# Recommendation scoring on one core: target rows fetched one by one from SyncE instead of by 128 indirect gathers on GpSimd

## Chip, cores and metric

The kernel runs on one core of a Trainium2 chip. The metric is the device time of one execution in microseconds (us). The median of 3 runs of the kernel before is 36,285.59 us (36,284.45 to 36,299.23).

## The reference

All arithmetic is in float32. There are 50,001 items, 16,384 users, and 100 history items for each user.

```python
def _neighbor_attn(E, near_full):                 # E: 50001 x 32
    V = E[near_full]                              # 32 neighbours of each item
    scores = jnp.einsum('nd,nkd->nk', E, V) / jnp.sqrt(jnp.float32(GEO_HALF))
    w = jax.nn.softmax(scores, axis=-1)
    return jnp.einsum('nk,nkd->nd', w, V)
...
a_sus = _neighbor_attn(E_in, near_full)
a_inf = _neighbor_attn(E_out, near_full)
hist_bi = jnp.concatenate([a_sus[history], a_inf[history]], axis=-1)
tgt_bi = jnp.concatenate([a_inf[target], a_sus[target]], axis=-1)
h = jnp.concatenate([E_hist[history], hist_bi], axis=-1)    # 16384 x 100 x 128
t = jnp.concatenate([E_tgt[target], tgt_bi], axis=-1)       # 16384 x 128
x = h * t[:, None, :]
z = jax.nn.relu(jnp.einsum('bld,hd->blh', x, W1) + b1)
scores = jnp.einsum('blh,h->bl', z, W2[0])
exp_A = jnp.exp(scores)
mask = (history != target[:, None]) & (history != 0)
exp_A = exp_A * mask
denom = jnp.sum(exp_A, axis=-1) ** BETA
attn = exp_A / denom[:, None]
result = h * attn[..., None]
s = jnp.sum(result)
...                                               # cosine of the vector (s, ..., s) and t
return jax.nn.sigmoid(pred)
```

## The kernel before

There are two stages, one behind the other, and both are paced by indirect gathers that GpSimd (POOL) issues. An indirect gather takes a column of 128 item numbers from SBUF and fetches one row of a DRAM table into each of the 128 partitions.

The first stage works out the neighbour attention of all items, 128 items at a time, with 32 gathers for each (L136), and writes two tables to DRAM: `table`, a row for an item as history (its sum and 128 values), and `ttab`, a row for an item as target (128 float32 values, 512 bytes; the first half is copied from the input at the very start, L104 and L105, and the second half is written by ScalarE's queue at the end of each block, L230).

The second stage scores the users. User number p x 128 + c lies in partition p of column c, so that the targets, loaded once as `tidx`, are a tile of 128 x 128 with the users' columns side by side, and `tidf` is the same in float32. There are 128 columns of 128 users. A column has 25 groups of four history positions. The order of the work is written out by hand (`tc.manual_schedule`) for all five engines, and each engine goes through its own work in that order:

- `history_of(i)` loads the histories of four columns from SyncE (SP), L292. There are 4 buffers.
- `target_rows(c)` fetches the target rows t of a column, L296. It is called for the first column ahead of the loop, and for each next column at group 5 of the one before. There are 3 buffers of t.
- `gather(s)` issues the four gathers of group s into one of HBUF = 20 buffers of `h`, L332.
- `turn(s)` transposes the four on PE, L346, and `times_target(s)` multiplies with the transposed target rows on DVE, L351, and sets the rows' sums aside, L354. When both have read a buffer of h, it is free for the gathers of group s + 20.
- `hidden` and `scored` are the two matrix products (L363, L372), three and six groups later, with the ReLU on ScalarE between them (L365).
- `target_work(c + 1)` transposes the next column's t on PE (L308), copies it (L310), sums it (L312) and its squares (L314), and makes the mask; it stands behind group 15 of column c. On PE, all groups that follow stand behind the transpose of t.
- `kept`, `turned_back`, `weights` and `ended` close a column.

SP's part of the second stage is the history loads alone: two ahead of the loop, and one at each fourth column.

Of the kernel before, what the change touches and what calls it, by code (L numbers as in the profile page):

```python
# [10 lines left out]
F32 = mybir.dt.float32  # L11
I32 = mybir.dt.int32
U8 = mybir.dt.uint8
E = mybir.EngineType
AF = mybir.ActivationFunctionType
ALU = mybir.AluOpType
AX = mybir.AxisListType

P = 128
ITEMS = 50001  # L20
# [3 lines left out]
D = 128  # L24
# [17 lines left out]
UC = B // P  # L42
# [3 lines left out]
W = 1 + D  # L46
LAG = 3
HBUF = 20

@with_exitstack
def kernel(
# [13 lines left out]
    nc = tc.nc  # L67
# [4 lines left out]
    const = ctx.enter_context(tc.tile_pool(name="const", bufs=1))  # L72
# [5 lines left out]
    ttab = dram.tile([ROWS, D], F32, name="ttab")  # L78

    ident = const.tile([P, P], F32, name="ident")  # L80
# [25 lines left out]
    with (  # L106
# [7 lines left out]
        its = {}  # L114
# [151 lines left out]
    tidx = const.tile([P, UC], I32, name="tidx")  # L266
    nc.scalar.dma_start(tidx, target.rearrange("(p c) -> p c", p=P))
    tidf = const.tile([P, UC], F32, name="tidf")
    nc.vector.tensor_copy(tidf, tidx)
    with (  # L270
        tc.manual_schedule(engines={E.PE, E.Activation, E.DVE, E.SP, E.Pool}),
        tc.tile_pool(name="u_1", bufs=1) as u_1,
        tc.tile_pool(name="u_in", bufs=4) as u_in,
        tc.tile_pool(name="u_t", bufs=3) as u_t,
        tc.tile_pool(name="u_h", bufs=HBUF) as u_h,
        tc.tile_pool(name="u_x", bufs=6) as u_x,
# [16 lines left out]

        def target_rows(c):
            t = u_t.tile([P, D], F32, name="t")
            nc.gpsimd.indirect_dma_start(  # L296
                out=t,
                out_offset=None,
                in_=ttab[0:ITEMS, :],
                in_offset=bass.IndirectOffsetOnAxis(ap=tidx[:, c : c + 1], axis=0),  # L300
            )
            users[c] = {"t": t, "hidx": hists[c // BSUB][:, c % BSUB, :]}

        def target_work(c):
# [103 lines left out]
        history_of(0)  # L408
        history_of(1)
        target_rows(0)  # L410
        target_work(0)
        for s in range(last + 2 * LAG + 8):
            c, g = divmod(s, NG)
            if s < last:
                if g == 0 and c % BSUB == 2 and 0 < c // BSUB and c // BSUB + 1 < UC // BSUB:
                    history_of(c // BSUB + 1)
                if g == 5 and c + 1 < UC:
                    target_rows(c + 1)
                gather(s)
                turn(s)  # L420
                times_target(s)
            if 0 <= s - LAG < last:
                hidden(s - LAG)
            if 0 <= s - 2 * LAG < last:
                scored(s - 2 * LAG)
            if s < last and g == 15 and c + 1 < UC:
                target_work(c + 1)
            done, left = divmod(s - 2 * LAG - NG, NG)
            if 0 <= done < UC and left == 0:
                kept(done)  # L430
            if 0 <= done < UC and left == 2:
                turned_back(done)
            if 0 <= done < UC and left == 4:
                weights(done)
            if 0 <= done < UC and left == 6:
                ended(done)

    with (
# [12 lines left out]
        s = f_s.tile([P, 1], F32, name="s")  # L451
# [72 lines left out]
```

## Time and profile before

| | |
|---|---|
| median of 3 runs | 36,285.59 us |
| span of the profiled execution, first to last instruction | 31,861.9 us |
| first stage, to the change at about | 15,690 us |
| POOL busy | 24,005.6 us, 75% of the span |
| PE busy | 11,868.8 us, 37% of the span, all but 0.5 us of it in the second stage |
| gathers on POOL | 12,512 (L136), 12,800 (L332), 128 (L296) |
| TensorE clock granted, mean | 0.905 |

The page gives the span of the profiled execution and no time of that execution beyond it; the runs' times are those of other executions, without the profiler. Lines are those of the kernel before. A group of instructions is given as: line, engine, operation, output and inputs, count; then busy time in us and the mean of one in ns; then the idle time of that engine just before these instructions, and what ended it. Instructions that issue transfers, load registers or branch are not counted as busy; SP and the queues of the other engines (SPq, ACTq) appear in the timeline and among the waits only.

### The profile page before, as it was taken

Reading aid. Unit: us, or ns where it says so; the run is one execution under the profiler, and the core shown is the slowest. Engines: PE = TensorE matmul, PEld = TensorE weight load, DVE = VectorE, ACT = ScalarE, POOL = GpSimd, SP = SyncE. Lnnn points to the kernel's source line nnn. Section 1 sums busy time; section 2 is a strip of 40 time slices with the busy share of each in tenths; the row PEclk is TensorE's granted clock in tenths of the full one; section 3 lists DMA queues with packets and bytes.
Section 4 is the critical chain, followed back from the end, with each engine's and each line's share of the span. In section 5 each row is a group of like instructions: output and inputs, shape, how many; then the busy total and the mean of one; then the engine's idle time right before and its main releaser. Section 6 shows DMA issues by size and latency. Waiting matters only on the chain.

```text
span 31861.9 us, 106268 instructions
## 1 busy us (share of the span) xinstructions
PE 11868.8 (37%) x26243; PEld 3178.4 (10%) x26243; DVE 6716.4 (21%) x11111; ACT 2745.2 (9%) x6067; POOL 24005.6 (75%) x25446
## 2 busy tenths in 40 slices
PE   0000000000000000000277777777777777777777
PEld 0000000000000000000011111111111111111111
DVE  2222222222222222222211111111111111111111
ACT  0000000000000000000011111111111111111111
POOL 7777777777777777777777777777777777777777
PEclk9999999999999999999988888888888888888888
DMA  2111111111111111111122222222222222222222
GB/s 50 30 30 30 30 31 33 30 30 30 30 31 33 30 30 30 30 31 31 37 54 54 54 54 54 54 54 54 54 54 54 54 54 54 54 54 54 54 53 52
DMA packets 1027971, 1362.44 MB, mean 43 GB/s; under 512 B 559904, under 2 KB 614432, under 8 KB 1027360
## 3 DMA queue, kind: packets, MB, share of 16 engines
q0 software_dynamic: 814080, 1265.42, 19.7%
q10 hardware_dynamic: 151056, 51.51, 1.0%
q1 hardware_dynamic: 62224, 38.72, 0.5%
q8 instruction: 217, 3.56, 0.0%
q14 instruction: 394, 3.23, 0.0%
HBM read 1315.31 MB, written 51.50 MB: 43 GB/s over the span
## 4 chain that ended last, share of the span: by engine, by line
POOL 56%; issue 27%; DMA 9%; PE 7%; DVE 1%; POOLq 0%; ACT 0%; ACTq 0%; SPq 0%; DVEq 0%
POOL v L136 35%; POOL h L332 21%; DMA h<-table,hidx 6%; PE turned L372 3%; DMA v<-in_egeo_dram,nidx 3%; PE z_ps L363 3%; PE hT_ps L346 1%; POOL t L296 0%; DVE xT L351 0%; DVE ea L404 0%; DVE den L403 0%; DVE num L405 0%; DVE ea L402 0%; DVE hsum L354 0%; DMA table<-row 0%
## 5 line engine op out<-in xcount | busy, mean ns | idle before, releaser
L332 POOL DMA_INDIRECT h<-table,hidx x12800 | 12080.4, 944 | 3901.8 <-issue 3587.3
L136 POOL DMA_INDIRECT v<-in_egeo_dram,nidx x12512 | 11803.8, 943 | 3860.2 <-issue 3723.3
L308 PE MATMUL hT_ps<-ident,t 128*128 128x128 f32 x128 | 46.7, 365 | 15689.8 <-DMA hidx<-in_history_dram 15689.8
L346 PE MATMUL hT_ps<-ident,h 128*128 128x128 f32 x12800 | 3926.4, 350 | 4284.2 <-DMA h<-table,hidx 4186.4
L351 DVE TENSOR_TENSOR xT<-hT_ps,tT 128x512 f32<-128x512 f32 x3200 | 2213.9, 692 | 13113.0 <-PE hT_ps L346 13109.7
L372 PE MATMUL turned<-z,w_row 128*25 128x512 f32 x6400 | 4560.1, 805 | 0.0
L363 PE MATMUL z_ps<-xT,w1T 128*128 128x512 f32 x6400 | 4300.2, 761 | 0.0
L365 ACT ACTIVATE z<-z_ps,b_sb 128x512 f32<-128x512 f32 x3200 | 2199.7, 687 | 13823.9 <-PE z_ps L363 13823.9
L153 DVE TENSOR_TENSOR big<-v,own_ps 128x2048 f32<-128x2048 f32 x391 | 897.9, 2296 | 11251.8 <-DMA v<-in_egeo_dram,nidx 11251.5
L346 PEld LDWEIGHTS hT_ps<-ident,h 128*128 128x128 f32 x12800 | 1779.4, 154 | 9334.4 <-DMA h<-table,hidx 5701.4
L308 PEld LDWEIGHTS hT_ps<-ident,t 128*128 128x128 f32 x128 | 19.2, 150 | 15842.7 <-issue 15841.9
L180 ACT ACTIVATE ex<-sc,top 128x32 f32<-128x32 f32 x782 | 227.7, 291 | 15155.2 <-DVE top L172 15142.5
L363 PEld LDWEIGHTS z_ps<-xT,w1T 128*128 128x128 f32 x6400 | 1343.1, 255 | 3.1 <-ACT z L365 3.1
L194 DVE TENSOR_TENSOR big<-v,ex 128x1024 f32<-128x1024 f32 x782 | 960.6, 1228 | 355.5 <-ACT ex L180 342.0
L163 DVE TENSOR_REDUCE sc<-big 128x64 f32<-128x2048 f32 x391 | 896.4, 2293 | 13.4
L207 DVE TENSOR_REDUCE att<-big 128x64 f32<-128x2048 f32 x391 | 895.8, 2291 | 0.0
L372 PEld LDWEIGHTS turned<-z,w_row 128*25 128x25 f32 x6400 | 458.8, 115 | 3323.6 <-issue 3323.6
L354 DVE COPY hsum<-h 128x4 f32<-128x4 f32 x3200 | 528.5, 165 | 0.0
L296 POOL DMA_INDIRECT t<-ttab,tidx x128 | 120.8, 943 | 66.0 <-issue 37.8
L180 ACT ACTIVATION_READ_ACCUMULATOR ex<-sc,top 128x1 f32 x782 | 145.8, 186 | 0.0
L310 DVE COPY tT<-hT_ps 128x128 f32<-128x128 f32 x128 | 37.4, 292 | 262.4 <-PE hT_ps L308 262.4
L214 DVE TENSOR_TENSOR row<-att,tot 128x64 f32<-128x64 f32 x391 | 88.2, 226 | 13.3
(55 smaller groups left out, 1008.1 us busy)
## 6 DMA issues: line engine op xcount, KB each, us to landing
h<-table,hidx POOLq DMA_INDIRECT x12800, 2.6
v<-in_egeo_dram,nidx POOLq DMA_INDIRECT x12512, 2.4
table<-row ACTq DMA_DIRECT2D x22, 1096.5 KB, 13.4
own<-in_egeo_dram SPq DMA_DIRECT2D x23, 544.0 KB, 4.0
row<-in_ehist_dram SPq DMA_DIRECT2D x23, 544.0 KB, 4.9
ttab<-in_etgt_dram ACTq DMA_DIRECT2D x1, 12500.0 KB, 54.2
ttab<-row ACTq DMA_DIRECT2D x22, 544.0 KB, 4.6
hidx<-in_history_dram SPq DMA_DIRECT2D x32, 200.0 KB, 2.5
```

What stands on the lines that cost most here:

```text
L136: nc.gpsimd.indirect_dma_start(out=v[:, k].rearrange("p t d -> p (t d)"), out_offset=None, in_=egeo, in_offset=bass.IndirectOffsetOnAxis(a ...
L153: nc.vector.tensor_tensor(prod.rearrange("p k t d -> p k (t d)"), v.rearrange("p k t d -> p k (t d)"), subs[s]["own"].to_broadcast([P, K, ...
L163: nc.vector.tensor_reduce(sc.rearrange("p t k -> p k t"), subs[s]["prod"], AX.X, ALU.add)
L194: nc.vector.tensor_tensor(subs[s]["wv"][:, t].rearrange("p d k -> p k d"), subs[s]["v"][:, :, t, :], subs[s]["ex"][0][:, t, :] .rearrange( ...
L207: nc.vector.tensor_reduce(att, subs[s]["wv"], AX.X, ALU.add)
L332: nc.gpsimd.indirect_dma_start(out=rows[s][:, q, :], out_offset=None, in_=table, in_offset=bass.IndirectOffsetOnAxis(ap=users[c]["hidx"][: ...
L346: nc.tensor.transpose(hT[s][:, q, :], rows[s][:, q, 1:W], ident)
L351: nc.vector.tensor_tensor(xT[s], hT.pop(s), users[c]["tT"].to_broadcast([D, LG, P]), ALU.mult)
L354: copy = nc.vector.tensor_copy(users[c]["hsum"][:, g * LG : (g + 1) * LG], rows.pop(s)[:, :, 0:1].rearrange("p q o -> p (q o)"),)
L363: nc.tensor.matmul(z_ps, w1T, xT.pop(s), start=True, stop=True)
L365: nc.scalar.activation(z[s], z_ps, AF.Relu, bias=b1_sb)
L372: nc.tensor.matmul(users[c]["turned"], w2_row[:, NG - 1 - g : 2 * NG - 1 - g], of.rearrange("h q p -> h (q p)"), start=g == 0, stop=g == N ...
```

## The change

Target rows are fetched by SP instead of POOL. Ahead of the second stage the targets' table is turned on PE, so that the 128 targets of column c lie side by side in partition c, and DVE multiplies them by the 512 bytes of a row and writes them as integers to `tat`. `target_rows(c)` then loads sixteen byte offsets at a time from `tat` into registers of SP, and starts sixteen transfers, each of one row of `ttab` into one partition of t, at the address that the register gives. That is 128 transfers and 8 loads of sixteen values for a column, 16,384 transfers in all, where there were 128 gathers. The division by 4 turns the byte offset into an offset in elements, and the bounds that stand with it tell the compiler that the offset is a multiple of 512.

```diff
@@ -46,6 +46,7 @@
 W = 1 + D
 LAG = 3
 HBUF = 20
+RUN = 16
@@ -267,6 +268,12 @@
     nc.scalar.dma_start(tidx, target.rearrange("(p c) -> p c", p=P))
     tidf = const.tile([P, UC], F32, name="tidf")
     nc.vector.tensor_copy(tidf, tidx)
+    tat = const.tile([UC, P], I32, name="tat")
+    with tc.tile_pool(name="tps", bufs=1, space=bass.MemoryType.PSUM) as tps:
+        tat_ps = tps.tile([UC, P], F32, name="tat_ps")
+        nc.tensor.transpose(tat_ps, tidf, ident)
+        nc.vector.tensor_scalar(tat, tat_ps, float(4 * D), None, ALU.mult)
+    ttab_flat = ttab.rearrange("(o n) d -> o (n d)", o=1)
     with (
         tc.manual_schedule(engines={E.PE, E.Activation, E.DVE, E.SP, E.Pool}),
         tc.tile_pool(name="u_1", bufs=1) as u_1,
@@ -293,12 +300,22 @@
         def target_rows(c):
             t = u_t.tile([P, D], F32, name="t")
-            nc.gpsimd.indirect_dma_start(
-                out=t,
-                out_offset=None,
-                in_=ttab[0:ITEMS, :],
-                in_offset=bass.IndirectOffsetOnAxis(ap=tidx[:, c : c + 1], axis=0),
-            )
+            for p in range(0, P, RUN):
+                _, at = nc.values_load_multi_w_load_instructions(
+                    tat[c : c + 1, p : p + RUN],
+                    engines=[E.SP],
+                    min_val=0,
+                    max_val=(ITEMS - 1) * 4 * D,
+                    skip_runtime_bounds_check_because="an item's number, times its row's bytes",
+                )
+                for q, v in enumerate(at):
+                    v = v.with_bounds(
+                        min_val=0,
+                        max_val=(ITEMS - 1) * 4 * D,
+                        guaranteed_mod_val=0,
+                        out_of_modulus=4 * D,
+                    )
+                    nc.sync.dma_start(t[p + q : p + q + 1, :], ttab_flat[:, ds(v // 4, D)])
             users[c] = {"t": t, "hidx": hists[c // BSUB][:, c % BSUB, :]}
```

## The prediction

> **What bounds the kernel now.** I read the head of the page first, then the groups by line, then the windows of the two stages.
>
> ```profile
> span 31861.9 us, 106268 instructions
> PE 11868.8 (37%) x26243; PEld 3178.4 (10%) x26243; DVE 6716.4 (21%) x11111; ACT 2745.2 (9%) x6067; POOL 24005.6 (75%) x25446
> POOL 56%; issue 27%; DMA 9%; PE 7%; DVE 1%; POOLq 0%; ACT 0%; ACTq 0%; SPq 0%; DVEq 0%
> ```
> ```profile
> L332 POOL DMA_INDIRECT h<-table,hidx x12800 | 12080.4, 944 | 3901.8 <-issue 3587.3 <-PE turned L372 159.1 <-PE hT_ps L346 97.8
> L136 POOL DMA_INDIRECT v<-in_egeo_dram,nidx x12512 | 11803.8, 943 | 3860.2 <-issue 3723.3 <-DMA v<-in_egeo_dram,nidx 128.4 <-DMA nidx<-in_near_dram 8.6
> L296 POOL DMA_INDIRECT t<-ttab,tidx x128 | 120.8, 943 | 66.0 <-issue 37.8 <-DVE w_row L286 27.3 <-DMA h<-table,hidx 0.6
> ```
> ```profile
> 8000.00:12000.00 4000.00, 0.00 (x0) 0.00 (x0) 1013.75 (x906) 105.27 (x600) 3015.73 (x3198) 1.00 0.17 31
> 20000.00:24000.00 4000.00, 2935.04 (x6504) 785.64 (x6504) 681.84 (x1873) 576.61 (x921) 3023.77 (x3204) 0.81 0.25 54
> ```
>
> POOL is busy 75%, yet it never rests: the other quarter is the 0.30 us between two gathers, which the groups book as "issue", a wait for nothing that the profile shows. In the chain of waits POOL and issue together carry 83% of the span. One gather of L332 costs (12080.4 + 3901.8) / 12800 = 1.249 us of POOL, busy and gap. The windows (columns: PE, PEld, DVE, ACT and POOL busy with their counts, granted clock, DMA share, GB/s) show the same number of gathers in 4000 us of either stage, 3198 and 3204, though DMA share and traffic differ. In the second stage PE is busy 2935 of 4000 us, 73%, so it follows POOL. A column of 128 users takes 100 gathers of L332 and one of L296; the former alone are 100 x 1.249 = 124.9 us.
>
> **What is removed.** L296 holds POOL 120.8 + 66.0 us, of which 27.3 us before the first gather wait for the stage change, and stay. The remaining (186.8 - 27.3) / 128 = 1.246 us is the price of one. The first of the 128 is free now, as the stage change shows (start, duration, engine, line, operation):
>
> ```profile
> 15682.45 1.25 ACTq L233 DMA_DIRECT2D table<-row  x1
> 15691.93 0.10 DVE L285 MEMSET w_row<- 128x49 f32 x1 [11.37 <-DMA table<-row]
> 15692.17 1.96 SPq L292 DMA_DIRECT2D hidx<-in_history_dram  x4
> 15692.71 0.94 POOL L296 DMA_INDIRECT t<-ttab,tidx  x1 [27.32 <-DVE w_row L286]
> 15694.87 0.94 POOL L332 DMA_INDIRECT h<-table,hidx  x1 [1.22 <-DMA hidx<-in_history_dram]
> 15696.12 0.94 POOL L332 DMA_INDIRECT h<-table,hidx  x1 [0.30 <-issue]
> ```
>
> The first h gather waits for its history until 15694.87 with or without L296 ahead of it. So 127 x 1.246 = 158 us leave POOL, and as POOL is the pace, they leave the span. Nothing on POOL comes in their place: the h gathers need the history and the table, not the target rows.
>
> **What is added at the stage change.** One PE transpose and one scaling by DVE, like these two:
>
> ```profile
> L93 PE MATMUL w_ps<-ident,w_sb 128*128 128x128 f32 x1 | 0.4, 446 | 6.6 <-DMA w_sb<-in_w_dram 6.6
> L94 DVE COPY w1T<-w_ps 128x128 f32<-128x128 f32 x1 | 0.3, 282 | 0.0
> ```
>
> That is 0.73 us. Their PSUM bank may be free only when the first stage's last sums are read; even then DVE idles 11.37 us behind the table write (L285 above), which hides them. Without that cover they cost under 2 us. I take nothing.
>
> **What is added on SP.** 128 row transfers a column and 8 loads of sixteen registers. Call x the time that one row takes SP, loads included; a column then takes T = 128x. SP has nothing else to do but 32 history loads, and its waits are those of a queue that ran ahead:
>
> ```profile
> SPq L292 <- DMA h<-table,hidx: 14109.1, 84, 506.4
> SPq L124 <- DMA ttab<-in_etgt_dram: 51.8, 1, 51.8
> ```
> ```profile
> 0.75 0.38 SPq L85 DMA_DIRECT2D b_sb<-in_b_dram  x1
> 1.19 0.42 SPq L87 DMA_DIRECT2D w_sb<-in_w_dram  x1
> 1.66 0.55 SPq L89 DMA_DIRECT2D w_sb<-in_w_dram  x1
> 2.25 0.44 SPq L119 DMA_DIRECT2D nidx<-in_near_dram  x1
> 2.73 0.44 SPq L121 DMA_DIRECT2D own<-in_egeo_dram  x1
> 54.96 0.65 SPq L124 DMA_DIRECT2D row<-in_ehist_dram  x1
> 55.65 1.70 SPq L119 DMA_DIRECT2D nidx<-in_near_dram  x1
> 57.40 0.43 SPq L121 DMA_DIRECT2D own<-in_egeo_dram  x1
> 57.88 0.56 SPq L124 DMA_DIRECT2D row<-in_ehist_dram  x1
> ```
> ```profile
> 31859.12 0.35 SPq L468 DMA_DIRECT2D out_dram<-res  x1
> ```
> ```profile
> h<-table,hidx POOLq DMA_INDIRECT x12800, 2.6
> ...
> hidx<-in_history_dram SPq DMA_DIRECT2D x32, 200.0 KB, 2.5
> ```
>
> The issue itself: transfers back to back start (2.73 - 0.75) / 4 = 0.50 us apart, the four histories 1.96 / 4 = 0.49. I take 0.49, though these have fixed addresses and no row here reads one from a register. The load of registers: no row shows one. It must fetch from memory and return, for which the nearest row is a whole transfer, 2.5 us to landing; one such trip for sixteen rows is 0.16 us a row. So x = 0.65 and T = 83 us. The bounds are 0.35 (the shortest issue, loads free) and 1.70 (the longest issue), T = 45 to 218 us.
>
> One wait may come on top. The ninth or so transfer of the program, L124, waited 51.8 us for a transfer of L104/L105 with which it shares no data, so the transfers share a small set of completion counts, and each new one waits for an old one to land. Seven were out by then (five on SP, two on ACT). With seven in flight and 2.5 us to landing that allows one every 0.36 us, below x. Behind a waiting row transfer on SP stand only later rows and the histories, which are wanted columns later.
>
> When is T short enough? POOL has 20 buffers of h, each a group of four gathers, so it runs 80 gathers, 99.9 us, past the point where PE stops. PE stops at the column's target transpose: for column 0 at the start, for column 1 behind its group 15. So POOL first stalls if T is over 99.9, or if 2T is over 36 x 4 x 1.249 = 179.9 us; later columns are less tight as long as T is under 124.9. At T = 83 neither happens. The buffers of t (three) let SP run over three columns ahead once it is ahead. Between x = 0.70 and 0.976 there is one stall of 2T - 180, at most 70 us, and the gain is 158 to 88 us.
>
> The Trainium skill has a price for the load in "DMA: Bandwidth & Descriptors", "Latency and other measured facts": a tensor_load takes no less than about 600 ns. One such load for sixteen rows would make x 0.49 + 0.04 = 0.53, no change to the sum; one for each row would make it 1.09, the second case below. No run here shows which.
>
> **Traffic.** The rows' packets join the gathers' on the same 16 engines (columns: packets, MB, share of the 16 engines).
>
> ```profile
> q1 hardware_dynamic: 62224, 38.72, 0.5%
> ```
> ```profile
> 53.71 0.94 POOL L136 DMA_INDIRECT v<-in_egeo_dram,nidx  x1 [0.30 <-issue]
> 54.96 0.94 POOL L136 DMA_INDIRECT v<-in_egeo_dram,nidx  x1 [0.30 <-issue]
> 56.21 0.94 POOL L136 DMA_INDIRECT v<-in_egeo_dram,nidx  x1 [0.30 <-issue]
> 57.46 0.94 POOL L136 DMA_INDIRECT v<-in_egeo_dram,nidx  x1 [0.30 <-issue]
> ```
>
> A packet of SP's queue took 0.005 x 16 x 31861.9 / 62224 = 41 ns. If each row is cut over all 16 engines, 16 pieces and 16 completions, that is 16384 x 32 x 41 ns / 16 = 1.34 ms an engine, 8% of the 16 ms: the share goes from 25% to 33%. And POOL's pitch stays 1.25 us while SP issues four transfers beside it, at 54.96 to 58.44. I cost this at nothing. The bounds are -2 ns a gather, the difference of the two windows (4000 / 3204 against 4000 / 3198, with the busier DMA the faster), and, an estimate, +31 ns, a tenth of the 0.30 gap.
>
> **The sum** for the profiled execution: -158 + 0 + 0 + 0. Its span is 31,861.9 us, the median of the runs 36,285.6; the 4,424 us between them stand in no row. If they are fixed, the gain stays 158; if they are a slower pitch, 36285.6 / 25440 = 1.426 us a gather, it is 181. I take 170: **36,115 us**.
>
> **The rivals.**
>
> *SP becomes the pace (slower).* If SP spends a second step as long as an issue on every row, an address or a register load of its own, x = 2 x 0.55 = 1.10 and T = 141. Then the last column's rows come at 128T, and PE has 34 groups left, at 2935 / (3204 / 4) = 3.66 us some 125 us. The cost is 128 x (140.8 - 124.9) + 125 - 158 = +2,002 us: 38,290. It decides from x = 0.978. For it: twice the usual issue is enough, and the longest row of SP, 1.70, is far beyond. Against it: six of the nine rows above are at or under 0.55. Chance 0.21.
>
> *The small packets slow the gathers (slower).* Each ns on an h gather costs 12.8 us, so from 12.4 ns, 1% of the pitch, nothing is left of the gain. At 31 ns it is 397 - 158 = +239: 36,525. Against it stand the two windows with equal counts at 31 and 54 GB/s. Chance 0.08.
>
> *Nothing is gained.* The row path is just at the edge, x near 0.98, or the gathers are slower by 7 to 18 ns: within 0.2%, or 73 us, about what a measurement of this kernel can tell from no change. 36,285. Chance 0.07.
>
> **How the numbers follow.** The forecast, x under 0.976 with an undisturbed POOL, has 0.64: faster. Nothing gained is the same, 0.07. The two others make slower, 0.29. The range starts at 36,285.6 - 181 = 36,105, less 10 for the -2 ns a gather, of which no more than a part is likely: 36,095. Upwards it holds the whole of the forecast, no gain, the packet case and of SP's case what lies under x = 1.02 (128 x 5.7 + 125 - 158 = +697): 37,000. What is left out is the rest of SP's case, 0.17, and little below. The likeliest sign's own range is 36,095 to 36,200.
>
> **What would show it.** Right: no L296 on POOL; L332 still 944 ns with 0.30 gap; in SP's timeline a row every 0.5 to 0.9 us with stretches in which SP waits for PE or ACT to release t; the first transpose of t some 85 us after the histories, and PE idle until then while POOL goes on. Wrong: POOL waiting for PE's transposes in every column, PE waiting for t's transfers throughout, SP never waiting for a release: then SP is the pace, and the column time divided by 128 is x. If POOL's gather is over 956 ns or its gap over 0.32 us, the packets did it.

## The result, and the profile after

After: 36,502.13 us, median of 4 runs (36,493.18 to 36,510.49); before, beside it, 36,292.41 us (36,284.45 to 36,299.24). The ratio is 1.0059, with a 95% interval of 1.0047 to 1.007: slower by 210 us where 170 us of gain were forecast. The time lies in the range; the sign is wrong.

One fact of the runs is needed to read this. The kernel before, unchanged, took 31,828 to 31,832 us on three of the chips used here and 36,180 to 36,313 us on two others. I call them the first and the second kind of chip; whether it is the chip itself or something that goes with it, no run tells. The profile of before in the prediction, with its span of 31,861.9 us, is of the first kind; the runs that were timed beside it, and the profile of after, are of the second. The section on the time before calls the runs' times those of executions without the profiler. But every run of after and of the experiments has a span and a granted clock of its own on record, and its span is 1.7 to 1.9 us under its time. So the 4,424 us between 31,861.9 and 36,285.6 us don't lie around the execution, but inside it.

The page of after, head and SP's queue:

```profile
span 36494.9 us, 141555 instructions
PE 10142.3 (28%) x26244; PEld 3175.6 (9%) x26244; DVE 6653.6 (18%) x11112; ACT 2689.2 (7%) x6067; POOL 25277.5 (69%) x25318
...
q1 hardware_dynamic: 94992, 47.18, 0.5%
```

Its groups by line (busy us, mean ns | idle before and what ended it), then its windows (PE, PEld, DVE, ACT, POOL, granted clock, DMA share, GB/s):

```profile
L137 POOL DMA_INDIRECT v<-in_egeo_dram,nidx x12512 | 13200.5, 1055 | 4296.3 <-issue 4187.5 <-DMA v<-in_egeo_dram,nidx 100.6 <-DMA nidx<-in_near_dram 8.2
L349 POOL DMA_INDIRECT h<-table,hidx x12800 | 12076.3, 943 | 6855.0 <-issue 5634.5 <-PE hT_ps L363 572.4 <-remote 343.4
```
```profile
8000.00:12000.00 4000.00, 0.00 (x0) 0.00 (x0) 911.48 (x815) 94.73 (x540) 3027.96 (x2856) 1.00 0.13 27
...
20000.00:24000.00 4000.00, 2164.35 (x5559) 675.37 (x5559) 569.58 (x1603) 481.55 (x788) 2560.00 (x2714) 0.73 0.18 46
```

The 128 gathers of the old L296 are gone, and a gather of h still takes 943 ns. But the idle time ahead of them has grown from 3901.8 to 6855.0 us, and the first stage, whose code the change doesn't touch, makes 2856 gathers in 4000 us instead of 3198. So these two profiles can't be subtracted from one another. The kernel before has to be seen on a chip of the second kind, and the kernel after on one of the first.

### The profile page after: what moved, and what is told of

It is laid out like the page before. It is cut to its first block, busy times and chain, and to the rows that moved or that the text cites. A ratio compares the mean times of both kernels' runs of the same rounds, so it can differ in the third digit from the quotient of the medians.

```text
span 36494.9 us, 141555 instructions
## 1 busy us (share of the span) xinstructions
PE 10142.3 (28%) x26244; PEld 3175.6 (9%) x26244; DVE 6653.6 (18%) x11112; ACT 2689.2 (7%) x6067; POOL 25277.5 (69%) x25318
## 3 DMA queue, kind: packets, MB, share of 16 engines
q1 hardware_dynamic: 94992, 47.18, 0.5%
q14 instruction: 666, 5.46, 0.1%
## 4 chain that ended last, share of the span: by engine, by line
another core or an unknown queue 31%; PE 15%; issue 3%; ACT 3%; SPq 0%; DVE 0%; ACTq 0%; DMA 0%
PE z_ps L380 6%; PE turned L389 5%; PE hT_ps L363 3%; ACT z L382 3%; SPq L318 0%; DVE xT L368 0%; PE hT_ps L325 0%; PE score L404 0%; ACT by_g L399 0%; SPq L304 0%; ACT junk L331 0%; DVE hsum L371 0%; ACT ea L412 0%; DVE ea L421 0%
## 5 line engine op out<-in xcount | busy, mean ns | idle before, releaser
L349 POOL DMA_INDIRECT h<-table,hidx x12800 | 12076.3, 943 | 6855.0 <-issue 5634.5
L137 POOL DMA_INDIRECT v<-in_egeo_dram,nidx x12512 | 13200.5, 1055 | 4296.3 <-issue 4187.5
L368 DVE TENSOR_TENSOR xT<-hT_ps,tT 128x512 f32<-128x512 f32 x3200 | 2193.7, 689 | 15700.7 <-remote 10366.7
L389 PE MATMUL turned<-z,w_row 128*25 128x512 f32 x6400 | 4112.0, 731 | 0.0
L382 ACT ACTIVATE z<-z_ps,b_sb 128x512 f32<-128x512 f32 x3200 | 2151.3, 686 | 16504.4 <-remote 11256.0
L363 PE MATMUL hT_ps<-ident,h 128*128 128x128 f32 x12800 | 2367.7, 314 | 512.0 <-DVE xT L368 428.4
L380 PEld LDWEIGHTS z_ps<-xT,w1T 128*128 128x128 f32 x6400 | 1200.1, 235 | 8416.1 <-ACT z L382 7099.2
L363 PEld LDWEIGHTS hT_ps<-ident,h 128*128 128x128 f32 x12800 | 1540.0, 156 | 3680.4 <-issue 2896.4
L371 DVE COPY hsum<-h 128x4 f32<-128x4 f32 x3200 | 559.3, 175 | 0.0
L325 PE MATMUL hT_ps<-ident,t 128*128 128x128 f32 x128 | 48.1, 376 | 216.6 <-DMA t<-ttab 207.8
```

Of the source, the lines that this page charges most:

```text
L137: nc.gpsimd.indirect_dma_start(out=v[:, k].rearrange("p t d -> p (t d)"), out_offset=None, in_=egeo, in_offset=bass.IndirectOffsetOnAxis(a ...
L349: nc.gpsimd.indirect_dma_start(out=rows[s][:, q, :], out_offset=None, in_=table, in_offset=bass.IndirectOffsetOnAxis(ap=users[c]["hidx"][: ...
L363: nc.tensor.transpose(hT[s][:, q, :], rows[s][:, q, 1:W], ident)
L368: nc.vector.tensor_tensor(xT[s], hT.pop(s), users[c]["tT"].to_broadcast([D, LG, P]), ALU.mult)
L371: copy = nc.vector.tensor_copy(users[c]["hsum"][:, g * LG : (g + 1) * LG], rows.pop(s)[:, :, 0:1].rearrange("p q o -> p (q o)"),)
L380: nc.tensor.matmul(z_ps, w1T, xT.pop(s), start=True, stop=True)
```

## Experiments: before on the second kind of chip

**e0_before** is before, without an edit.

> The kernel before, unchanged, for a second profile: the first one has a span of 31,862 us, the timed runs take 36,290. If the timed runs have a pause or a slower pitch that the first profile lacks, the span is near 36,290, the first stage takes about 17,500 us as in the profile of the changed kernel (15,690 in the first profile), and the profile shows which instructions are longer. If the 4,424 us lie around the span, the span is 31,862 again.

Measured: 36,179.79 us, one run. The span is near the time and the first stage is the long one: the first of the two cases that were expected. Its page, two groups and two windows:

```profile
span 36178.0 us, 106268 instructions
```
```profile
L136 POOL DMA_INDIRECT v<-in_egeo_dram,nidx x12512 | 13208.4, 1056 | 4286.3 <-issue 4180.4 <-DMA v<-in_egeo_dram,nidx 98.2 <-DMA nidx<-in_near_dram 7.7
L332 POOL DMA_INDIRECT h<-table,hidx x12800 | 12106.3, 946 | 6329.5 <-issue 4998.3 <-remote 555.5 <-PE hT_ps L346 431.2
```
```profile
8000.00:12000.00 4000.00, 0.00 (x0) 0.00 (x0) 910.51 (x815) 94.70 (x540) 3025.65 (x2857) 1.00 0.13 27
20000.00:24000.00 4000.00, 2166.23 (x5664) 677.87 (x5664) 587.33 (x1633) 495.13 (x802) 2629.20 (x2781) 0.73 0.19 47
```

The first stage is as slow as in after (2857 against 2856 gathers; there POOL's gathers themselves take longer, 1,056 and 1,055 ns instead of 943). So the 1,868 us that after loses in it (first row transfer of the second stage at 17,529 us, and at 15,661 in a1_after, the same kernel on a chip of the first kind) belong to the chip. In the second stage before, too, has long idle times ahead of its gathers, only less of them: 2781 gathers in the window, one in 101 of them a gather of t, against 2714. What such an idle time is, the timeline of after shows (start, duration, engine, line, operation, idle before and its end):

```profile
24003.17 0.66 PE L363 MATMUL hT_ps<-ident,h 128*128 128x128 f32 x4
24003.18 32.84 SPq L318 DMA_DIRECT2D t<-ttab  x21
...
24003.66 1.02 PE L380 MATMUL z_ps<-xT,w1T 128*128 128x512 f32 x2
...
24022.20 0.69 DVE L368 TENSOR_TENSOR xT<-hT_ps,tT 128x512 f32<-128x512 f32 x1 [17.49 <-remote]
...
24027.81 0.69 ACT L382 ACTIVATE z<-z_ps,b_sb 128x512 f32<-128x512 f32 x1 [19.64 <-remote]
24028.31 0.95 POOL L349 DMA_INDIRECT h<-table,hidx  x1 [0.31 <-issue]
24028.55 0.50 PEld L380 LDWEIGHTS z_ps<-xT,w1T 128*128 128x128 f32 x2 [16.29 <-ACT z L382]
24028.55 2.07 PE L380 MATMUL z_ps<-xT,w1T 128*128 128x512 f32 x2 [16.05 <-ACT z L382]
...
24034.24 0.69 DVE L368 TENSOR_TENSOR xT<-hT_ps,tT 128x512 f32<-128x512 f32 x1 [11.22 <-PE hT_ps L363]
...
24034.92 0.68 DVE L368 TENSOR_TENSOR xT<-hT_ps,tT 128x512 f32<-128x512 f32 x1
...
24035.58 0.68 DVE L368 TENSOR_TENSOR xT<-hT_ps,tT 128x512 f32<-128x512 f32 x1
24035.75 0.94 POOL L349 DMA_INDIRECT h<-table,hidx  x1 [6.49 <-issue]
```

DVE, ACT and PE stand still for 16 to 20 us here, with work ready: the transposes that L368 reads at 24022.20 had ended at 24003.83, the products that L382 reads at 24027.81 at 24004.68. Then they do one or two things each before the next pause; SP gets 21 rows out in 33 us. POOL alone keeps its pitch, until its 20 buffers are full and nobody empties them; then it stops as well, here for 6.49 us. Near the end of that stop the others come back (three L368 within 2 us), and it begins anew. I call this a stop.

The buffers are the reason of POOL's own standstill in every stop of after that the table counts: all 20 are held when it begins, and it ends 0.74 us (at most 1.06) after DVE's L371 has read the oldest of them. That read comes 5.1 us into the stop in the median, though PE had transposed the same buffer 23 us before. Counted from POOL's records, gaps of over 3 us between 18.5 and 36 ms:

| kernel | added on SP over the second stage | stops | mean us | sum us |
|---|---|---|---|---|
| e0_before | nothing | 383 | 5.73 | 2,195 |
| e1_rows_once | nothing past column 0 | 394 | 5.73 | 2,256 |
| e2_half | 17,408 instructions, 8,192 of them transfers | 435 | 5.40 | 2,347 |
| c5_wait | 32,768 waits, 128 transfers | 435 | 5.27 | 2,292 |
| c4_fixed | 16,384 instructions, all transfers | 449 | 5.67 | 2,548 |
| e3_both | 33,792 instructions, 16,384 of them transfers | 483 | 5.18 | 2,502 |
| c6_after40 | as after | 492 | 5.46 | 2,685 |
| after | 33,792 instructions, 16,384 of them transfers | 501 | 5.39 | 2,702 |

On chips of the first kind no profile has a single one; from the 500th gather of h on, none of the twelve has even a gap over 0.4 us. The kernels with more on SP have more stops; the experiments below take that apart. The limit of 3 us hides a part of it. From the 500th gather on, gaps of 1 to 3 us make 371 us in c5_wait and 207 in e1_rows_once. With them counted, the gaps over 1 us hold the whole difference between e1, c5, c4 and after (2,489, 2,698, 2,839 and 2,939 us); the gathers themselves take the same in all four (11,605 to 11,612 us).

## Experiments: what the change's parts cost there

**e1_rows_once**: the gathers removed, rows fetched for column 0 alone, and kept. It is the floor: the gain without the price.

```diff
+            if c > 0:
+                users[c] = {"t": kept_t[0], "hidx": hists[c // BSUB][:, c % BSUB, :]}
+                return
-            t = u_t.tile([P, D], F32, name="t")
+            t = u_1.tile([P, D], F32, name="t")
+            kept_t[0] = t
```

> The target rows of column 0 are fetched by SP once and used for all columns, so that from column 1 on neither SP nor POOL fetches any (the output is that of wrong targets). This is the floor under the change. Theory A, SP is too slow for a column and sets the pace (its rows are 1.14 us apart in the changed kernel's profile): 36,290 - 127 x 1.42 = 36,110 us. Theory B, each row transfer on SP slows the other engines by its mere presence: 36,110 too. If it stays near 36,500, neither holds and the cost is in the turned table or in the order of the waits.

**e2_half**: half of the transfers, of two rows each (every second target is left out, its neighbour's next row comes in its place); all loads stay.

```diff
                 for q, v in enumerate(at):
+                    if q % 2:
+                        continue
...
-                    nc.sync.dma_start(t[p + q : p + q + 1, :], ttab_flat[:, ds(v // 4, D)])
+                    nc.sync.dma_start(
+                        t[p + q : p + q + 2, :],
+                        ttab_flat[:, ds(v // 4, 2 * D)].rearrange("o (r d) -> (o r) d", d=D),
+                    )
```

> The changed kernel with 64 transfers a column instead of 128, each of two rows of the table that lie one behind the other into two partitions (every second target is wrong, the bytes are the same). Theory A: SP needs 64 x 1.14 = 73 us a column, half of what the others need, so the time falls all the way to the floor, about 36,110. Theory B: half of the excess over the floor stays, (36,502 + 36,110) / 2 = 36,306.

**e3_both**: before with its gathers, and SP's rows beside them into a tile that nobody reads. `spare_rows` is the changed loop of `target_rows`.

```diff
+            t = u_t.tile([P, D], F32, name="spare")
...
         def target_rows(c):
...
+            spare_rows(c)
             users[c] = {"t": t, "hidx": hists[c // BSUB][:, c % BSUB, :]}
```

> The kernel before with its 128 gathers, and the 16,384 row transfers on SP beside them, into a tile that nobody reads. Theory A: no engine waits for SP's rows, so the time is that of before, 36,290, or, if SP is behind at the end or late with the histories, that of the changed kernel at most, 36,502. Theory B: the transfers cost the other engines what they cost in the changed kernel, 36,502 - 36,110 = 392 us: 36,680.

Measured, against before at 36,192.26 us: e1 36,040.71 us, 0.9958 (0.9941 to 0.9974); e2 36,189.65 us, 0.9999 (0.999 to 1.0009); e3 36,494.21 us, 1.0083 (1.0066 to 1.01). The window of e3, whose POOL count holds the gathers of t too:

```profile
20000.00:24000.00 4000.00, 2171.89 (x5539) 674.62 (x5537) 566.24 (x1598) 480.99 (x785) 2582.62 (x2738) 0.73 0.19 46
```

Taking the gathers away gains 152 us on this kind of chip also. Fetching the rows by SP costs 302 us even where no engine waits for them, so the cost isn't a wait for rows. Half of the transfers cost about 149 us over the floor, near half. Theory A of these expectations, SP's own pace, falls with both. Theory B held in kind, but its sizes were too large: it had a gain of 180 us for e1, a cost of 392 for e3 and half of that for e2.

Next, which part of SP's work costs: **c4_fixed** keeps the transfers and drops loads and address moves (rows at fixed addresses, so other rows than the targets'); **c5_wait** is e1 with waits that are always met and touch no memory, merged by the compiler to 256 a column, and one small transfer a column to hold SP in step; **c6_after40** is after with twice the h buffers.

```diff
c4_fixed
+            for p in range(P):
+                r = (c * P + p) * 37 % ITEMS
+                nc.sync.dma_start(t[p : p + 1, :], ttab[r : r + 1, :])
c5_wait, on top of e1
+            mark = u_t.tile([1, P], F32, name="mark")
+            nc.sync.dma_start(mark, ttab[c : c + 1, :])
+            for _ in range(4 * P):
+                nc.sync.wait_ge(spin, 0)
c6_after40
-HBUF = 20
+HBUF = 40
```

> Rows once, with 32,768 instructions on SP that wait for nothing and 128 transfers. Where before takes 31,830: 0.995. Where it takes 36,200 or so: B1 (each transfer costs) 0.996, B2 (each instruction costs) 1.006.

> Fixed rows, 16,384 transfers with one instruction each. Where before takes 31,830: 0.995. Where it takes 36,200 or so, theory F, both cost: the 32,768 instructions without transfers came to 1.0012 against a floor of 0.9958, 0.0054, or 0.0027 for 16,384; the rest of the changed kernel's 0.0101, 0.0047, is the transfers'. So 0.9958 + 0.0027 + 0.0047 = 1.003. B1 (transfers alone) 1.006, B2 (instructions alone) 1.001.

> The changed kernel with 40 buffers of h. Where before takes 31,830: 0.995. Where it takes 36,200 or so: theory C (too little slack) 0.93 to 0.97, theory D (the others stand still until POOL stops) 1.006.

Measured: c5 36,225.76 us, 1.0012 (1.0002 to 1.0021) against 36,185.58; c4 36,360.62 us, 1.0011 (1.0001 to 1.0021), and c6 36,546.46 us, 1.0063 (1.0046 to 1.0079), both against 36,313.37. The waits added in c5, by source line (duration ns min/median/max):

```profile
L309 SPq EVENT_SEMAPHORE  x32647: 1/28/1421, 17530.0 to 35757.8; - x200
```

An instruction that starts no transfer, 28 ns long and off every engine's path, costs time. Neither theory fits alone: c5 lies between the 0.996 of B1 and the 1.006 of B2, and c4 came out at the 1.001 of B2, under the 1.003 of theory F, which its interval leaves out. By the ratios, and with e1 as the floor, c5 lies (1.0012 - 0.9958) x 36,190 = 195 us over it, c4 192 us and after (1.0059 - 0.9958) x 36,292 = 366 us. A part of this falls at the stage change, as the section on the prediction shows: by the 500th gather of the second stage c5 is 41 us later than e1, after 40 us later, c4 9 us and e2 14 us earlier. The rest gives two prices: (195 - 41) / 32,768 = 4.7 ns for an instruction, and (192 + 9) / 16,384 = 12.3 ns for an instruction with its transfer, so 7.6 ns for a transfer. That takes a move or a load to cost what a wait costs, which no run shows. They are then held against runs that didn't make them: e2 17,408 x 4.7 + 8,192 x 7.6 = 144 us, measured 149 + 14 = 163; e3 33,792 x 4.7 + 16,384 x 7.6 = 283 us, measured 302, of which 9 by the 500th gather. So, on this reading, instructions and transfers both cost, each near half of the whole. The prices rest on the floor of one chip; by the intervals of the ratios they are uncertain by some 2 ns for an instruction and 3 for a transfer.

One more thing comes with an instruction: it has to be loaded. The pages count the packets of a queue that they call "instruction", here of e0_before and of c5_wait:

```profile
q14 instruction: 394, 3.23, 0.0%
...
q14 instruction: 653, 5.35, 0.1%
```

After has 666 of them, and so has a1_after, where nothing stops. The price above is that of an instruction with its loading; these runs don't separate the two. A stop doesn't need a load, though: of the 500 stretches of after from the end of one stop to the end of the next, 107 hold no packet of instructions on either of the two queues of that kind.

More buffers don't help: the stops of c6 come as often as those of after and are as long (492 and 501, 5.46 and 5.39 us; median distance 35.5 us in both), and all 40 buffers are held when each of them begins. So theory C is refuted. Of theory D the time came about, and "half as often and twice as long", as the expectation of e6_after40 below puts it, did not.

## Experiments: the first kind of chip

**a1_after** is after, unchanged.

> The changed kernel again, unchanged. Where the kernel before takes 31,830 us (no stops of POOL, as on the chip of the runs with fixed rows and with 40 buffers), theory E says that the prediction's sum holds: SP needs 128 x 0.323 + 8 x 1.2 = 51 us a column, nothing waits for it, and 127 gathers go, 31,830 - 158 = 31,672 (0.995). Where the kernel before takes 36,180 to 36,290, it is 1.006 to 1.008 of it again. The rival to E, that the transfers of target rows cost the same on every chip, says 1.006 or more on both.

Measured: 31,673.01 us against 31,828.08, 0.9951 (0.9934 to 0.9968). The change gains 155 us here. Its page, groups, instructions of two lines, waits of SP, timeline of the stage change, and a window:

```profile
span 31671.9 us, 141555 instructions
```
```profile
L349 POOL DMA_INDIRECT h<-table,hidx x12800 | 12078.9, 944 | 3931.5 <-issue 3190.9 <-DMA h<-table,hidx 230.3 <-PE turned L389 210.0
```
```profile
L318 SPq MOVE t<-ttab x16384: 29/29/38, 15661.3 to 31156.9; - x200
L318 SPq DMA_DIRECT2D t<-ttab x16384: 227/228/340, 15661.4 to 31157.0; - x200
```
```profile
L304 SPq TENSOR_LOAD <-tat x1024: 1134/1256/1546, 15660.1 to 31150.2; - x171
```
```profile
SPq L318 <- DVE tsum L329: 8668.1, 122, 73.7
```
```profile
15661.38 58.14 SPq L318 DMA_DIRECT2D t<-ttab  x144
15714.74 0.45 PE L325 MATMUL hT_ps<-ident,t 128*128 128x128 f32 x1 [70.27 <-DMA t<-ttab]
```
```profile
20000.00:24000.00 4000.00, 2953.81 (x6569) 789.07 (x6568) 688.40 (x1890) 582.04 (x929) 3023.07 (x3205) 0.82 0.22 54
```

A row takes SP 0.323 us, a move of 29 ns and a transfer of 228 ns among it; the load of sixteen takes 1.256 us. SP then waits for the release of t in nearly every column, 8,668 us in all, and POOL keeps its 0.307 us between gathers and its 3205 of them in the window.

The three kernels c4_fixed, c5_wait and c6_after40 were run on three chips of this kind too, under the labels e, a and b, and e7_before40 is before with `HBUF = 40`:

> The 16,384 row transfers from fixed rows: no registers are loaded or moved, so SP has one instruction a row instead of 2.06 (the rows are not the targets'). Floor (rows once) is 0.9958 of before, the changed kernel 1.0059. Theory B1, each transfer costs: 1.006 of before. Theory B2, each instruction that SP goes through costs, transfer or not: 0.9958 + 0.0101 / 2.06 = 1.001. Theory A, SP's own pace, predicts the floor.

> Rows once, and in every column SP goes through 256 instructions that wait for nothing (two waits for zero each), one transfer of a row, and DVE copies that row: 32,768 instructions on SP, as many as the changed kernel has, and no transfers but 128. Theory B1: the floor, 0.9958 of before (36,140). Theory B2: 1.0059 of before.

> The changed kernel with HBUF = 40 instead of 20 buffers of h. In its profile POOL stops every 35 us for some 6 us, when PE, ScalarE, DVE and SP have stood still for some 25 us and all 20 buffers are full. Theory C, the stops are too little slack: with 40 buffers POOL runs through most of them, and up to 2,600 us go (its stops in the second stage), 0.93 to 0.97 of before. Theory D, the others stand still until POOL stops: they then stand still longer, POOL's stops come half as often and twice as long, and the time stays at 1.006 of before.

> The kernel before with HBUF = 40. Theory C: up to 2,200 us go (POOL's stops in its second stage), 0.94 to 0.97 of before. Theory D: 1.000 of before.

> The fixed rows again. Where before takes 31,830: 0.995, as before. Where it takes 36,200 or so: B1 (each transfer costs) 1.006, B2 (each instruction on SP costs) 1.001.

> Rows once, with 32,768 instructions on SP that wait for nothing. Where before takes 31,830: 0.995. Where it takes 36,200 or so: B1 0.996, B2 1.006.

> The changed kernel with 40 buffers of h. Where before takes 31,830: 0.995. Where it takes 36,200 or so: theory C (too little slack) 0.93 to 0.97, theory D (the others stand still until POOL stops) 1.006.

> Fixed rows, 16,384 transfers with one instruction each. Where the kernel before takes 31,830: 0.995. Where it takes 36,200 or so, with the stops: B1 (each transfer costs) 1.006, B2 (each instruction on SP costs) 1.001.

> Rows once, with 32,768 instructions on SP that wait for nothing and 128 transfers. Where before takes 31,830: 0.995. Where it takes 36,200 or so: B1 0.996, B2 1.006.

> The changed kernel with 40 buffers of h. Where before takes 31,830: 0.995. Where it takes 36,200 or so: theory C (too little slack) 0.93 to 0.97, theory D (the others stand still until POOL stops) 1.006.

| kernel | first chip | second | third |
|---|---|---|---|
| before beside it | 31,831.95 | 31,828.08 | 31,829.56 |
| fixed addresses | 31,677.36, 0.9952 | 31,671.9, 0.9951 | 31,670.41, 0.995 |
| waits alone | 31,674.1, 0.9951 | 31,671.0, 0.9951 | 31,673.99, 0.9951 |
| after, 40 buffers | 31,676.76, 0.9951 | 31,671.65, 0.9951 | 31,672.44, 0.995 |
| before, 40 buffers | 31,831.04, 1.0 | | |

(Intervals: 0.9933 to 0.9968 over all the 0.99 ratios, 0.999 to 1.001 for the last.) What was to be told apart on a chip that stops could not be told apart here, since these chips never stop: whatever SP does, the gain is the 155 us of the gathers. That is a result too. 32,768 waits or 16,384 transfers on SP cost nothing measurable of their own (all medians with 127 gathers less lie from 31,670 to 31,677 us); they cost where the stops are. Of the versions that fetch the right rows for every column, none beat after on the first kind by more than 2 us, and none beat before on the second.

## Why the prediction was right and wrong

**What bounds the kernel; what is removed: right.** 127 gathers at 1.246 us are 158 us. Measured are 155 us on the first kind of chip and 152 us (e1) on the second. The Trainium skill says in "DMA: Bandwidth & Descriptors", "Issuing engines are not separate DMA queues", that issuing from several engines saves only the sequencer's time, usually small beside the transfer. Here it was not small: POOL spent 1.246 us on a gather that landed 2.6 us after its issue, and as POOL is the pace, that time was the whole gain, 0.49% of the kernel.

**What is added on SP: right in kind, mis-sized both ways.** x was put at 0.49 + 0.16 = 0.65 us and T at 83 us. On the first kind of chip a row takes 0.323 us and its share of a load 1.256 / 16 = 0.08 us, so x = 0.40 and T = 52 us; no stall, as forecast, and the first transpose 55 us behind the histories instead of 85. The Trainium skill, in "DMA: Bandwidth & Descriptors", "Latency and other measured facts", puts a tensor_load at no less than about 600 ns; the trace agrees, at 1.256 us for sixteen values.

On the second kind T is far larger. Row starts of after give 141.9 us for the mean column and 4.1 us between columns, x = 1.14, while SP's own instructions wait little for other transfers:

```profile
L318 SPq DMA_DIRECT2D t<-ttab x16384: 1/228/1424, 17529.0 to 36214.2; - x200
```
```profile
SPq L318 <- DMA t<-ttab: 133.5, 232, 1.8
```

The transfer's median is the same 228 ns; but from one row to the next it takes 0.725 us in the median, not 0.323, and 543 of the steps are over 3 us: SP is slowed with the others. For column 0 the first transpose came 136 us after the first row. The prediction's own bound for a stall was 99.9 us, and the stalls are there, the second of them in column 1 (timeline of after, PE and POOL):

```profile
17665.00 0.45 PE L325 MATMUL hT_ps<-ident,t 128*128 128x128 f32 x1 [156.33 <-DMA t<-ttab]
17668.30 0.94 POOL L349 DMA_INDIRECT h<-table,hidx  x1 [38.21 <-PE hT_ps L363]
17783.18 0.45 PE L325 MATMUL hT_ps<-ident,t 128*128 128x128 f32 x1 [51.44 <-DMA t<-ttab]
17786.47 0.94 POOL L349 DMA_INDIRECT h<-table,hidx  x1 [31.11 <-PE z_ps L380]
```

136 - 99.9 = 36 us were to be expected of the first, and 38.21 came. After them the rows are ahead: SP issues the last row of a column 48 us before its transpose in column 8, 120 us in column 64.

**SP becomes the pace: not so, though near.** x = 1.14 is over the 0.978 at which that rival was to decide. But the same stops stretch POOL's column, 100 gathers at 1.474 us on the mean, to 147.4 us, which puts the point at 1.15. Of PE's waits for t, 156.33 + 51.44 of 207.8 us fall in the two columns above; past them PE doesn't wait for t, and the +2,002 us didn't come:

```profile
L325 PE MATMUL hT_ps<-ident,t 128*128 128x128 f32 x128 | 48.1, 376 | 216.6 <-DMA t<-ttab 207.8
```

c4_fixed, whose rows pause for 61.6 us between one column and the next, costs 192 us over the floor all the same.

**Traffic: costed at nothing by the wrong measure.** The mechanism of that rival, slower gathers, is refuted: 943 ns each, and 1.249 us in the median from one to the next. The sign that the prediction gave for it, a gap over 0.32 us, would have misled: the mean gap of after is 6855.0 / 12800 = 0.54 us, but that of e0_before, which has no rows on SP, is 0.49. The packets were 94,992 - 62,224 = 32,768, two for each row, not 32. In the second stage DMA share went from 25% to 22% on the first kind of chip. Yet the transfers have a price through the stops, 7.6 ns each.

**The sum: this is the step that failed.** "Its span is 31,861.9 us, the median of the runs 36,285.6; the 4,424 us between them stand in no row. If they are fixed, the gain stays 158; if they are a slower pitch ... 181." Either way the step took them as something that the change leaves alone. Of the 4,316 us between the spans of e0_before and of the prediction's profile, 1,834 lie ahead of the first gather of h, where POOL's own gathers are slower, and there the change does nothing. The other 2,482 lie in the second stage. They are the stops, which the profile at hand did not hold, and how many there are depends on what SP does. For the removed gathers "fixed" came near (e1 gained 152 us, not 181); for the work on SP, which stands in the sum as 0, neither did. So a term was left out that had no place in that profile: 33,792 instructions x 4.7 ns + 16,384 transfers x 7.6 ns = 283 us. With it: -152 (e1) + 40 (stalls at the stage change beyond those of e1) + 283 = +171 us, against +210 measured. The 39 us that are left are about the half-width of the ratio's interval, 0.00115 x 36,292 = 42 us; whether they are more than that stays open.

Open as well is why the chips of the second kind stop, and by what an instruction of SP that does nothing brings the next stop nearer. The runs show that it does (a stop each 40.1 us in c5_wait, each 46.3 in e1_rows_once, medians), and that DVE comes back once POOL has stood still for some 5 us; they don't show what the engines wait for. That would need a kernel whose POOL can be slowed at will beside a fixed load of SP; it wasn't tried. Nor do they exclude that the recording of the traces has a part in the stops. In the time that the table counts, the traces hold 206 to 231 instructions for each stop in seven of the kernels, and 255 in c5_wait, all engines counted: within a quarter of each other, while SP's part goes from almost none to 31,900 of 112,000. A run without a recording would decide it, and none of the runs of after and of the experiments is one.

## What to carry to other kernels

When the profiled span and the timed runs lie apart as here, 31,862 and 36,286 us, the profile is of another regime, and a forecast from its rows holds for that regime alone: the difference has to be treated as an unknown that the change can alter, in both signs. Work moved to an engine that idles isn't free by that alone; ask how many instructions it has, since here the idle engine got 33,792 for 128 that were removed, and a few ns on each undid a gain of 150 us. A buffer depth, 80 gathers here, gives the bound for a late start, and it held to 2 us in a regime that was not foreseen.

## What the hardware showed unexpectedly

- The same kernel took 31,830 or 36,180 to 36,313 us depending on the chip. On the slower chips a gather of the first stage took 1,055 ns instead of 943. In the second stage POOL stopped for more than 3 us in every 35 to 47 us; DVE, ACT and PE stood still for 16 to 20 us in the stretch shown, and came back near the end of POOL's stop.
- There, 32,768 waits on SP that were always met made the kernel 154 us longer besides the stage change; on the other chips nothing measurable (31,671 to 31,674 us, where after took 31,673).
- A row of 512 bytes at an address from a register made two packets, one of 512 bytes and one of 4, and took SP 0.323 us: 29 ns for the move, 228 ns for the transfer, the rest between them. Sixteen registers were loaded in 1.256 us.
